# One-hots of a counting sort stored and reloaded, high rows loaded a group ahead, four count buffers, and a later first node piece

## The chip, the cores and the metric

The kernel runs on one core of one Trainium2 chip. A core has five engines that each execute their own queue in order: TensorE (PE, with its weight loads PEld), VectorE (DVE), ScalarE (ACT), GpSimd (POOL) and SyncE (SP, which here issues most plain DMAs). DMAs move the data between DRAM and the on-chip memory; those that gather or scatter rows by an index list are issued by POOL, one instruction for 128 rows. The metric is the device time of one execution in microseconds (us), the median of three runs.

## The reference

A graph layer on 3125 nodes of 256 features. It has three parts:

```
xn = layernorm(x)
x  = x + gnn(xn, edge_attr, src, dst) + mix(xn)      # 103125 edges, sorted by dst
x  = x + ffn(layernorm(x), edge_index)               # 65536 other edges + one loop for each node

gnn:  msg = concat(nodes[src], edge_attr) @ W_message       # 320 -> 256
      agg = segment_sum(msg, dst)
      h = layernorm(relu(agg) + nodes); three-layer MLP with skips; layernorm
mix:  4 layers of (linear attention over all nodes; feed-forward 256 -> 1024 -> 256)
ffn:  h = x @ W_gat (16 columns); e = leaky_relu(a_src[src] + a_dst[dst])
      alpha = softmax of e over the edges of one dst; agg = segment_sum(h[src] * alpha, dst)
      scores = mean over heads of layernorm(agg + b_gat); the two best of 4 experts, softmax
      weighted sum of the experts' MLPs, all four computed densely
```

The 65536 edges of the last part are not sorted. The kernel sorts them by destination itself.

## The kernel before

**Message passing.** The 103125 edges lie as 128 partitions of 806 consecutive edges ("columns"). `gather_chunk` loads the attributes of 8 columns (L494, SP) into one of three buffers `m_run` and lets POOL gather the 128 source rows of each column (L515). `sum_up` (L527, DVE) adds a column to the running sum of its partition, and after the eighth column SP stores the chunk to `run_d` (L532). The chunk's buffer then takes the next gathers. After the last column, `message_nodes` fetches for each tile of 128 nodes the finished sum (`fetch`, L595, POOL, into `aggr`), and `pair` carries two tiles through transposes (L611), the message weights (L619, L620), layer norms and the MLP, in steps ("pieces").

**The sort.** The edges lie as 128 x 512, in 64 groups of GC = 8 positions. A destination is split into a high part (127 bins) and a low part (32 bins).

- `count_group(t)` builds one-hots of the high parts (`oh_hi`, L695) and the low parts (`oh_lo`, L701, made by `low_hots`, 64 KB in f16, three buffers) on DVE; eight matmuls (L716) give each position's count table; ACT casts it into one of two buffers `counts0`, `counts1` (L718); SP stores it to `counts_d` (L719); PE adds it to a table kept for the whole sort (L723). That last matmul is for the group counted one call before.
- `starts` turns the table into the place of each destination's first edge and loads the counts of the first group (`parts`, L732). `edge_ranges`, 25 `ends_tile`, `ends_sum` and `ends_done` find where each node's edges begin and end; `ends_tile` works in a buffer `ends_buf`.
- `place_group(t)` loads the high parts of the group's edges in transposed order, broadcast to all partitions (`hr`, 256 KB, two buffers, L756, SP), compares them with the partition number (`ohT`, L758, DVE), builds the low one-hots once more (`low_hots`, L701), runs a scan over the group's counts (L761) and orders the edges within the group by products of one-hots (L775, ACT's sign into `earlier`). In the next call the matmuls from L781 on (the first reads `oh_lo`), the product `own` and the sum L791 give each edge's number. Every fourth group, `laid` turns numbers into places.
- `send(t)` scatters 128 edges to their places (L805, POOL); there are 512.

**The mix** runs on PE, ACT and DVE beside all of this; `finish` ends it for four tiles, computes the GAT table `tab` (L859) and scatters the rows of a dst (L866, POOL). After it the rows of the sources are fetched in sorted order (L1291, 340 gathers into `rows_c`), and the rest of the last part ends the kernel.

**Order.** The program's text sets each engine's order through a planner's clock, and a scheduler in the compiler may still move what is not pinned. After each step of the mix, `pace(us)` moves the clock on, runs one waiting piece of the node stage, and writes as many columns (later sends) as the clock has room for at one each 1.27 us; columns are pinned in that order. `beside(us)` takes jobs of the sort from a list, each with a cost in planned time. When the last column is written, 24 sends go out and `message_nodes` is called.

```
    def pace(us):
        clock["now"] += us
        if pieces:
            piece()
        ...
        while clock["columns"] < TM and FIRST + COLUMN * (clock["columns"] + 1) <= clock["now"]:
```

Of the kernel before, what the change touches and what calls it, by code (L numbers as in the profile page):

```python
# [11 lines left out]
F16 = mybir.dt.float16  # L12
# [6 lines left out]
P = 128  # L19
# [21 lines left out]
TE = E2 // P  # L41
NEXP = 4
GC = 8
GROUPS = TE // GC
SRC = 4096
LO = 32
# [13 lines left out]
def kernel(ctx: ExitStack, tc: tile.TileContext, a: dict, out: bass.AP):  # L60
# [347 lines left out]
        V.tensor_scalar(above, node_n, -1.0, SRC // 2 - 0.5, op0=ALU.mult, op1=ALU.add)  # L408

    def ends_tile(t):  # L410
        buf = so.tile([P, 8 * P], F16, name="ends_buf", tag="hr", bufs=2)
        at_least = buf[:, 6 * P:7 * P]
        V.tensor_scalar(at_least, row0, start_t[:, t:t + 1], None, op0=ALU.is_ge)
        T.matmul(first_ps[:, t:t + 1], at_least, ones_h, start=True, stop=True, skip_group_check=True)
        le, own = buf[:, :P], buf[:, P:2 * P]
        V.tensor_scalar(le, ids, whole_t[:, t:t + 1], None, op0=ALU.is_ge)
        T.matmul(whole_ps[:, t:t + 1], le, ones_h, start=True, stop=True, skip_group_check=True)
        V.scalar_tensor_tensor(own, ids, prev_t[:, t:t + 1], le, op0=ALU.is_ge, op1=ALU.subtract)
        for k, (c0, c1) in enumerate(((0, TM // 2), (TM // 2, TM))):
            ps = pa.tile([P, 512], F32, name="ps_a")  # L420
            T.matmul(ps[:, :c1 - c0], own, dst_h[:, c0:c1], start=True, stop=True)
            hit = buf[:, 2 * P:2 * P + TM // 2]
            S.activation(hit, ps[:, :c1 - c0], AF.Sign, bias=above[:, t:t + 1], accum_out=cnt2n[:, k, t:t + 1])
# [117 lines left out]


    FIRST, COLUMN, PIECE, EARLY = 52.0, 1.27, 0.9, 24
    clock = {"now": 45.0, "columns": 0, "sent": 0}

    pieces = []

# [4 lines left out]

    def pace(us):
        clock["now"] += us
        if pieces:
            piece()
        pinned = True
        while clock["columns"] < TM and FIRST + COLUMN * (clock["columns"] + 1) <= clock["now"]:
            sum_up(clock["columns"], pinned)
            pinned = False  # L560
            clock["columns"] += 1
            if clock["columns"] == TM:
                while clock["sent"] < min(EARLY, clock["placed"]):
                    send(clock["sent"])
                    clock["sent"] += 1
                for _ in range(len(jobs) - N_JOBS + ENDS):
                    jobs.pop(0)[1]()
                msgs.close()
                message_nodes()
        while (clock["columns"] == TM and clock["sent"] < clock["placed"]  # L570
               and FIRST + COLUMN * (TM + clock["sent"]) <= clock["now"]):
            send(clock["sent"])
            clock["sent"] += 1
# [125 lines left out]
    def low_hots(t):  # L699
        o = so.tile([P, GC, LO], F16, name="oh_lo", bufs=3)  # L700
        V.tensor_tensor(o, low_ids.rearrange("p (o l) -> p o l", o=1).to_broadcast([P, GC, LO]),  # L701
                        lo[:, t:t + GC].rearrange("p (t o) -> p t o", o=1).to_broadcast([P, GC, LO]), op=ALU.is_equal)
        return o

    counts_d = dram.tile([GROUPS, P, LO * (GC + 1)], F16, name="counts_d")
    counted = []
    cnts = [so.tile([P, LO, GC + 1], F16, name=f"counts{k}") for k in range(2)]
    for o in cnts:
        V.memset(o[:, :, 0], 0.0)

    def count_group(t):
        if t < TE:
            ohh, ohl = one_hot(t, hi, P, "oh_hi", 2), low_hots(t)
            ps = pg.tile([P, GC, LO], F32, name="ps_g")
            for i in range(GC):
                T.matmul(ps[:, i, :], ohh[:, :, i], ohl[:, i, :], start=i == 0, stop=i == GC - 1, skip_group_check=True)  # L716
            cnt = cnts[t // GC % 2]
            S.copy(cnt[:, :, 1:].rearrange("p l i -> p i l"), ps)  # L718
            nc.sync.dma_start(counts_d[t // GC, :, :], cnt.rearrange("p l i -> p (l i)"))  # L719
            counted.append((t, cnt))  # L720
        if t:
            t, cnt = counted.pop(0)
            T.matmul(table, ident_h, cnt.rearrange("p l i -> p (l i)"), start=t == 0, stop=t + GC == TE, skip_group_check=True)  # L723

    def split(x, near, rest):

        V.tensor_copy(near, x)
        V.tensor_tensor(rest[:, :, 0], x, near, op=ALU.subtract)
# [6 lines left out]
    def starts():  # L735
        cnt2 = so.tile([P, LO], F32, name="cnt2", tag="base")
        V.tensor_reduce(cnt2, table.rearrange("p (l i) -> p l i", i=GC + 1), AX.X, ALU.add)
        cum2 = so.tile([P, LO], F32, name="cum2", tag="oh_lo", bufs=3)
        V.tensor_tensor_scan(cum2, ones[:, :LO], cnt2, 0.0, op0=ALU.mult, op1=ALU.add)
        ps = pg.tile([P, LO], F32, name="ps_g")  # L740
        T.matmul(ps[:, :1], before, cum2[:, LO - 1:], start=True, stop=True)
        V.tensor_tensor(cum2, cum2, cnt2, op=ALU.subtract)
        base2 = so.tile([P, 1], F32, name="base2")
        V.tensor_copy(base2, ps[:, :1])
        V.tensor_scalar(cum2, cum2, base2, None, op0=ALU.add)
        nc.sync.dma_start(start_d, cum2)
        V.tensor_scalar(cum2, cum2, half, None, op0=ALU.add)
        places.append(parts(0))
        split(cum2, *places[0])

    def place_group(t):

        late = looks.pop() if looks else None
        if t < TE:
            hr = so.tile([P, GC, P], F16, name="hr", bufs=2)
            nc.sync.dma_start(hr.rearrange("p t e -> p (t e)"), row_h[t // GC:t // GC + 1, :].to_broadcast([P, P * GC]))  # L756
            ohT = ohTs[t // GC % 2]
            V.tensor_scalar(ohT[:P - 1], hr[:P - 1], bin_p[:P - 1], 2.0, op0=ALU.is_equal, op1=ALU.mult)  # L758
            ohl = low_hots(t)
            near, run_l = places.pop()  # L760
            V.tensor_tensor_scan(run_l.rearrange("p l i -> p (l i)"), goes.rearrange("p l i -> p (l i)"),  # L761
                                 run_l.rearrange("p l i -> p (l i)"), 0.0, op0=ALU.mult, op1=ALU.add)
            run = so.tile([P, GC, LO], F16, name="run_c", tag=f"counts{t // GC % 2}")
            S.copy(run, run_l[:, :, :GC].rearrange("p l i -> p i l"))
            if t + GC < TE:
                base = so.tile([P, LO], F32, name="base")
                V.tensor_tensor(base, run_l[:, :, GC], near, op=ALU.add)
                places.append(parts(t + GC))
                split(base, *places[0])

            earlier = so.tile([P, GC, P], F16, name="earlier", bufs=2)
            for i0 in range(0, GC, 4):
                ps = pt.tile([P, 4, P], F32, name="ps_t")
                for i in range(4):
                    T.matmul(ps[:, i, :], ohT[:, i0 + i, :], ohT[:, i0 + i, :], start=i == 0, stop=i == 3, skip_group_check=True)  # L775
                S.activation(earlier[:, i0:i0 + 4, :], ps, AF.Sign, bias=slope[:, 2:3], scale=slope[:, 1:2])  # L776
            looks.append((t, ohT, ohl, near, run, earlier))
        if late:
            t, ohT, ohl, near, run, earlier = late
            look = pg.tile([P, GC, LO], F32, name="ps_g")  # L780
            T.matmul(look, all_h, ohl, start=True, stop=False, skip_group_check=True)  # L781
            for k in range(3):
                for i in range(GC):
                    if k == 2:
                        a1, a2 = earlier[:, i, :], ohl[:, i, :]
                    else:
                        a1, a2 = ohT[:P - 1, i, :], run[:P - 1, i, :] if k else near[:P - 1]
                    T.matmul(look[:, i, :], a1, a2, start=False, stop=k == 2, skip_group_check=True)
            own = so.tile([P, GC, LO], F32, name="own_bin", bufs=1)
            V.scalar_tensor_tensor(own, look, float(E2), ohl, op0=ALU.add, op1=ALU.mult)  # L790
            V.tensor_reduce(number[t // SG % 2][:, t % SG:t % SG + GC], own, AX.X, ALU.add)  # L791
            if (t + GC) % SG == 0:
                V.tensor_scalar_mul(number[t // SG % 2], number[t // SG % 2], 0.5)
                laid(place[:, t + GC - SG:t + GC], number[t // SG % 2])
                clock["placed"] = t + GC

    places = []
    looks = []
    SG = 4 * GC
    number = [so.tile([P, SG], F32, name=f"number{i}") for i in range(2)]  # L800

# [900 lines left out]
```

## Time and profile before

| | us |
|---|---|
| three runs | 2485.49, 2495.59, 2499.51; median 2495.59 |
| the profiled execution | 2499.97, of which the span of the trace is 2498.3 |

| stage of the trace (us) | what runs in it |
|---|---|
| 34 to 145 | first gathers and columns, first layer of the mix begins |
| 145 to 340 | the 64 count groups, in three bursts, beside 124 gathers |
| 340 to 496 | starts, ranges, ends; 111 gathers |
| 496 to 1198 | place groups (36 of 64), the mix, 500 gathers; the last column ends at 1200.6 |
| 1198 to 1908 | 512 sends, 25 fetches of sums, the node stage, the other 28 place groups |
| 1908 to 1940 | last feed-forward matmul at 1918.7, the last scatters of the GAT table |
| 1940 to 2498 | 340 gathers of source rows (to 2417) and the tail |

How it is read. A line of the groups gives the source line, the engine, the operation, what it writes and reads, the number of instructions, then busy time and mean duration in ns, then the idle time of the engine just before these instructions and what ended it. For POOL, "issue" is time in which the engine waited for nothing that the profile shows; it comes with every DMA that POOL issues. A line of the waits gives the engine and line that waited, what released it, the sum in us, how often, and the longest. A line of a timeline begins with the start in us and the duration. A line of the windows view gives the stretch, its length, the busy time of PE, PEld, DVE, ACT and POOL, the granted TensorE clock, the busy share of the DMA engines, and GB/s.

### The profile page before, as it was taken

What the parts mean: (1) busy time and instruction counts of PE and PEld (TensorE: products, weight loads), DVE (VectorE), ACT (ScalarE), POOL (GpSimd) and SP (SyncE); (2) the same over time, 40 slices, a digit from 0 to 9 for tenths busy, and PEclk for the clock granted to TensorE, in tenths of its full rate; (3) what the DMA queues carried; (4) which work ended last, traced back from release to release, by engine and by line L of the source; (5) the groups of instructions that cost most, each with busy time, mean ns of one, the idle gap of its engine ahead of it and who ended that gap; (6) DMA issues with size and microseconds to landing.
All of it is one profiled execution on the core that took longest, in us unless ns stands there. A gap on an engine that the chain in (4) does not pass through costs nothing. (4 is left out here: it accounts for less than half of the span.)

```text
span 2498.3 us, 32120 instructions
## 1 busy us (share of the span) xinstructions
PE 2047.1 (82%) x10045; PEld 1417.0 (57%) x10045; DVE 1481.2 (59%) x4506; ACT 1168.8 (47%) x2040; POOL 1723.6 (69%) x1755
## 2 busy tenths in 40 slices
PE   3869778587879998879499988899999698888874
PEld 2656555365556666547276665666676455555544
DVE  7886876677777667678254434656442344444446
ACT  5646555345444444444255656556544132323234
POOL 4575667667767777766777777777776766666652
PEclk9979888797889998889699989999999898999987
DMA  8986778878987877877411112213110121211112
GB/s 256 313 255 215 247 216 274 209 253 258 304 263 260 262 264 238 294 256 247 144 30 37 37 34 55 73 45 82 45 26 8 23 47 21 48 21 31 23 21 61
DMA packets 302237, 361.80 MB, mean 145 GB/s; under 512 B 183324, under 2 KB 249205, under 8 KB 288853
## 3 DMA queue, kind: packets, MB, share of 16 engines
q1 hardware_dynamic: 233061, 244.77, 30.7%
q0 software_dynamic: 68992, 114.85, 16.9%
q8 instruction: 82, 1.34, 0.2%
q14 instruction: 102, 0.84, 0.1%
HBM read 203.45 MB, written 160.11 MB: 146 GB/s over the span
## 5 line engine op out<-in xcount | busy, mean ns | idle before, releaser
L515 POOL DMA_INDIRECT m_run<-xn_d,src_i x806 | 813.8, 1010 | 378.0 <-issue 211.9
L805 POOL DMA_INDIRECT by_dst<-pairs,place x512 | 502.5, 982 | 156.1 <-issue 154.3
L527 DVE SCALAR_TENSOR_TENSOR m_run<-m_run,stay 128x320 f32<-128x320 f32 x805 | 437.6, 544 | 73.4 <-DMA m_run<-xn_d,src_i 61.9
L1291 POOL DMA_INDIRECT rows_c<-tab_d,si x340 | 326.7, 961 | 150.2 <-issue 100.4
L1149 PE MATMUL ps_a<-h,w 128*128 128x512 f32 (+1 forms) x896 | 392.6, 584 | 6.2 <-ACT h L165 6.1
L1160 PE MATMUL ps_a<-w,gT 128*128 128x256 f32 x1600 | 366.3, 383 | 0.0
L1160 PEld LDWEIGHTS ps_a<-w,gT 128*128 128x128 f32 x1600 | 304.0, 192 | 49.1 <-issue 6.1
L1149 PEld LDWEIGHTS ps_a<-h,w 128*128 128x128 f32 x896 | 168.3, 207 | 167.1 <-issue 148.7
L1150 ACT ACTIVATE gT<-ps_a,b 128x512 f32<-128x512 f32 (+1 forms) x224 | 141.0, 637 | 137.9 <-PE ps_a L1149 136.0
L124 ACT ACTIVATE hn<-xm,rstd 128x256 f32<-128x256 f32 x225 | 120.9, 594 | 62.3 <-DVE rstd L120 58.2
L776 ACT ACTIVATE earlier<-ps_t,slope 128x512 f16<-128x512 f32 x128 | 93.9, 772 | 110.8 <-PE ps_t L775 110.4
L1284 DVE SCALAR_TENSOR_TENSOR ps_g<-tile_ids,high_of,ps_g 128x500 f32<-128x500 f32 x60 | 43.8, 740 | 169.4 <-PE ps_g L1283 168.3
L1410 ACT ACTIVATE hf<-ps_a,be 128x512 f32<-128x512 f32 (+1 forms) x112 | 69.9, 640 | 154.3 <-PE ps_a L1408 147.3
L1283 PE MATMUL ps_g<-tab_c,which 128*128 128x500 f32 x120 | 69.0, 700 | 67.0 <-DVE rows_c L1286 64.3
L160 PE MATMUL ps_t<-ident,hn 128*128 128x128 f32 x450 | 83.7, 320 | 47.3 <-ACT hn L124 41.5
L1087 PE MATMUL ps_g<-xm,kr 128*128 128x256 f32 x400 | 109.6, 412 | 11.8 <-ACT kr L1085 11.3
L1061 PE MATMUL ps_a<-wq,h 128*128 128x256 f32 x400 | 100.5, 394 | 20.8 <-ACT kT L1041 12.8
L1029 PE MATMUL ps_a<-h,wk 128*128 128x512 f32 (+1 forms) x224 | 103.7, 598 | 2.7 <-ACT h L165 2.7
L1087 PEld LDWEIGHTS ps_g<-xm,kr 128*128 128x128 f32 x400 | 78.6, 205 | 44.2 <-ACT kr L1085 29.0
L160 PEld LDWEIGHTS ps_t<-ident,hn 128*128 128x128 f32 x450 | 57.5, 159 | 81.3 <-ACT hn L124 59.6
L1138 PE MATMUL ps_a<-co,hT 128*128 128x256 f32 x400 | 99.3, 391 | 0.8 <-DVE co L1129 0.6
L718 ACT CAST counts<-ps_g 128x256 f16<-128x256 f32 x64 | 80.3, 1375 | 41.5 <-PE ps_g L716 21.4
(436 smaller groups left out, 3812.4 us busy)
## 6 DMA issues: line engine op xcount, KB each, us to landing
run_d<-m_run SPq DMA_DIRECT2D x100, 1280.0 KB
m_run<-in_edge_attr_dram SPq DMA_DIRECT2D x95, 256.0 KB
hr<-row_h SPq DMA_DIRECT2D x64, 256.0 KB
m_run<-xn_d,src_i POOLq DMA_INDIRECT x806
w<-in_L_mix_W_dram SPq DMA_DIRECT2D x8, 1024.0 KB
by_dst<-pairs,place POOLq DMA_INDIRECT x512
rows_c<-tab_d,si POOLq DMA_INDIRECT x340
run_d<-rows_c SPq DMA_DIRECT2D x15, 312.0 KB
```

Source lines behind the costliest of these rows:

```text
L124: S.activation(dst, src, AF.Identity, bias=r[:, 1, i:i + 1], scale=r[:, 0, i:i + 1])
L160: T.transpose(ps[:, i * P:(i + 1) * P], src[:, c * P:(c + 1) * P], ident)
L515: last_gather[0] = G.indirect_dma_start(out=m[:, t, :D], out_offset=None, in_=xn_d, in_offset=bass.IndirectOffsetOnAxis(ap=src_i[:, t0 + t ...
L527: add = V.scalar_tensor_tensor(m[:, t, :], before_m, stay[:, c:c + 1], m[:, t, :], op0=ALU.mult, op1=ALU.add)
L805: i = G.indirect_dma_start(out=by_dst, out_offset=bass.IndirectOffsetOnAxis(ap=place[:, t:t + 1], axis=0), in_=pairs0[:, t:t + 1], in_offs ...
L1029: T.matmul(ps[:, :n], att_w[l]["wk"][:, kc, m * P:(m + 1) * P], h1[:, kc, :n], start=kc == 0, stop=kc == 1)
L1061: T.matmul(ps[:, i, :], h1[:, kc, o + i * P:o + (i + 1) * P], att_w[l]["wq"][:, kc, :], start=kc == 0, stop=kc == 1)
L1087: T.matmul(ps_x[:, m, :], kr[:, m * P:(m + 1) * P], xm[:, t, :], start=i == 0 and m == 0, stop=i == len(c) - 1, skip_group_check=True)
L1149: T.matmul(ps[:, :w], ff_w[l]["w1"][:, kc, f * P:(f + 1) * P], h2[:, kc, :w], start=kc == 0, stop=kc == 1)
L1150: S.activation(gT[:, f, :w], ps[:, :w], AF.Gelu, bias=ff_w[l]["b1"][:, f:f + 1])
L1160: T.matmul(ps[:, i, :], gT[:, f, (2 * i0 + i) * P:(2 * i0 + i + 1) * P], ff_w[l]["w2"][:, f, :], start=False, stop=f == FF // P - 1, skip_ ...
L1291: G.indirect_dma_start(out=rows_c[:, t - COLS[j], :], out_offset=None, in_=tab_d, in_offset=bass.IndirectOffsetOnAxis(ap=si[:, t:t + 1], a ...
```

## The change

1. **Low one-hots.** `count_group` also stores its `oh_lo` to a DRAM tile `lows_d` (64 stores of 64 KB, 512 bytes for each partition). `place_group` no longer builds them; they are loaded from there.
2. **High rows.** The load of `hr` leaves `place_group`. A new `ahead_of(t)` loads `hr` and `oh_lo` of one group; `starts` calls it for the first two groups, and `place_group` calls it for the group after the next right after `own`. `ends_buf` uses the buffers of `earlier` instead of those of `hr`.
3. **Count buffers.** Four instead of two (the two new ones share the space of `run`), and the table matmul L723 follows two groups behind the counting instead of one; what is left is added at the end.
4. **Node stage.** When the columns are done, the pieces may start only once the planner's clock has moved on by 1.27 x (24 + 8) = 40.6 us. The pace (52.0 and 1.27) stays.

SP issues 128 more DMAs (1640 to 1768), and DVE 64 fewer one-hots. The order of columns against place groups is the same. Line numbers in the text are those of the kernel before.

```diff
     def ends_tile(t):
-        buf = so.tile([P, 8 * P], F16, name="ends_buf", tag="hr", bufs=2)
+        buf = so.tile([P, 8 * P], F16, name="ends_buf", tag="earlier", bufs=2)
...
     def pace(us):
         clock["now"] += us
-        if pieces:
+        if pieces and clock["now"] >= clock["fetched"]:
             piece()
...
                 message_nodes()
+                clock["fetched"] = clock["now"] + COLUMN * (EARLY + 8)
...
     cnts = [so.tile([P, LO, GC + 1], F16, name=f"counts{k}") for k in range(2)]
+    cnts += [so.tile([P, LO, GC + 1], F16, name=f"counts{k}", tag="run", bufs=2) for k in range(2, 4)]
+    lows_d = dram.tile([GROUPS, P, GC * LO], F16, name="lows_d")
...
-            cnt = cnts[t // GC % 2]
+            cnt = cnts[t // GC % 4]
             S.copy(cnt[:, :, 1:].rearrange("p l i -> p i l"), ps)
             nc.sync.dma_start(counts_d[t // GC, :, :], cnt.rearrange("p l i -> p (l i)"))
             counted.append((t, cnt))
-        if t:
-            t, cnt = counted.pop(0)
-            T.matmul(table, ident_h, cnt.rearrange("p l i -> p (l i)"), start=t == 0, stop=t + GC == TE, skip_group_check=True)
+            nc.sync.dma_start(lows_d[t // GC, :, :], ohl.rearrange("p t l -> p (t l)"))
+        while counted and (len(counted) > 2 or t >= TE):
+            now, cnt = counted.pop(0)
+            T.matmul(table, ident_h, cnt.rearrange("p l i -> p (l i)"), start=now == 0, stop=now + GC == TE, skip_group_check=True)
...
         split(cum2, *places[0])
+        for t in (0, GC):
+            ahead_of(t)
+
+    def ahead_of(t):
+        hr = so.tile([P, GC, P], F16, name="hr", bufs=2)
+        nc.sync.dma_start(hr.rearrange("p t e -> p (t e)"), row_h[t // GC:t // GC + 1, :].to_broadcast([P, P * GC]))
+        ohl = so.tile([P, GC, LO], F16, name="oh_lo", bufs=3)
+        nc.sync.dma_start(ohl.rearrange("p t l -> p (t l)"), lows_d[t // GC, :, :])
+        highs.append((hr, ohl))
...
         if t < TE:
-            hr = so.tile([P, GC, P], F16, name="hr", bufs=2)
-            nc.sync.dma_start(hr.rearrange("p t e -> p (t e)"), row_h[t // GC:t // GC + 1, :].to_broadcast([P, P * GC]))
+            hr, ohl = highs.pop(0)
             ohT = ohTs[t // GC % 2]
             V.tensor_scalar(ohT[:P - 1], hr[:P - 1], bin_p[:P - 1], 2.0, op0=ALU.is_equal, op1=ALU.mult)
-            ohl = low_hots(t)
...
             V.scalar_tensor_tensor(own, look, float(E2), ohl, op0=ALU.add, op1=ALU.mult)
+            if t + 2 * GC < TE:
+                ahead_of(t + 2 * GC)
```

More of the change, by code (lines that the diff above doesn't have):

```diff
@@ L543 @@
     FIRST, COLUMN, PIECE, EARLY = 52.0, 1.27, 0.9, 24
-    clock = {"now": 45.0, "columns": 0, "sent": 0}
+    clock = {"now": 45.0, "columns": 0, "fetched": 0.0, "sent": 0}
     pieces = []
@@ L798 @@
     looks = []
+    highs = []
     SG = 4 * GC
```

## The prediction

> **What bounds the kernel now.** I read the page first.
>
> ```profile
> PE 2047.1 (82%) x10045; PEld 1417.0 (57%) x10045; DVE 1481.2 (59%) x4506; ACT 1168.8 (47%) x2040; POOL 1723.6 (69%) x1755
> L515 POOL DMA_INDIRECT m_run<-xn_d,src_i x806 | 813.8, 1010 | 378.0 <-issue 211.9
> L805 POOL DMA_INDIRECT by_dst<-pairs,place x512 | 502.5, 982 | 156.1 <-issue 154.3
> ```
>
> POOL is busy for 69%, but "issue" is time between two of its DMAs that nothing could fill. A gather costs 1010 + 211.9/806 = 1.27 us with it, a send 1.28 us. The 806 gathers (34 to 1198 us) and then 512 sends (to 1908) follow each other with little else, so POOL's order is the path. Only its waits beyond "issue" can be won: 378.0 - 211.9 = 166.1 us for the gathers, 1.8 for the sends.
>
> Next, POOL's groups by stage: counting (145 to 340), the ranges (340 to 496), the first places (496 to 700), and the stage of the sends (1198 to 1940, last three lines).
>
> ```profile
> L515 POOL DMA_INDIRECT m_run<-xn_d,src_i x124 | 129.8, 1047 | 65.6 <-issue 33.5 <-DVE m_run L527 17.1 <-DMA counts_d<-counts 6.3
> L515 POOL DMA_INDIRECT m_run<-xn_d,src_i x111 | 108.5, 978 | 48.0 <-issue 28.0 <-DVE laid L682 9.8 <-DMA m_run<-xn_d,src_i 8.1
> L515 POOL DMA_INDIRECT m_run<-xn_d,src_i x141 | 141.9, 1007 | 61.6 <-issue 37.6 <-DMA run_d<-m_run 6.7 <-DVE run L761 6.3
> L805 POOL DMA_INDIRECT by_dst<-pairs,place x512 | 502.5, 982 | 156.1 <-issue 154.3 <-DMA by_dst<-pairs,place 0.9 <-DVE rstd L120 0.9
> L595 POOL DMA_INDIRECT aggr<-run_d,sum_i x25 | 24.2, 969 | 15.2 <-issue 5.2 <-PE ps_t L775 4.1 <-DMA run_d<-over,carry_i 3.3
> L866 POOL DMA_INDIRECT tgt_d<-tab,start_i x25 | 23.9, 958 | 16.6 <-DVE tab L859 9.6 <-issue 6.4 <-PE ps_a L1408 0.3
> ```
>
> Beyond issue POOL waits 65.6 - 33.5 = 32.1 us in counting, 20.0 and 24.0 in the next two stages; the same view gives 29.0 for 700 to 1076 and 16.5 for 1076 to 1198. That is 121.6 us, the most that the gathers can give after 145 us. The scatters L866 wait 9.6 us for the last table (L859), because PE's mix chain ends (1918.7 us) after the last send (1907.8).
>
> Last, the waits in counting (us in all, times, longest).
>
> ```profile
> PE sums_ps L723 <- ACT counts L718: 42.4, 46, 3.5
> DVE oh_hi L695 <- PE ps_g L716: 23.2, 32, 1.7
> ACT counts L718 <- DMA counts_d<-counts: 18.2, 13, 3.1
> POOL m_run L515 <- DVE m_run L527: 17.1, 6, 6.8
> ```
>
> PE, executing in order, stands at the table matmul (L723) for the cast of the group just counted; DVE then stands at the next one-hot for PE; column sums queued behind it on DVE come late; their chunk's buffer comes free late; POOL waits.
>
> **Counting: four count buffers, lagged table matmul, low one-hots stored.** The 64 groups run in three bursts (147-196, 221-276, 289-338 us), 151 us, or 2.36 us a group. The change removes the waits of 42.4 (the matmul is two groups behind) and 18.2 (a count buffer returns after four groups, not two). It adds 64 stores of 64 KB on SP and a wait: the low one-hot has three buffers, and one is now free only when its store has landed. DVE would stand there with high one-hots and columns behind it, and POOL behind those. No lows_d store is in the trace; the nearest row is the counts store, which ACT's casts wait for. ACT's timeline and SP's, first column the start:
>
> ```profile
> 169.74 2.50 ACT L718 CAST counts<-ps_g 128x256 f16<-128x256 f32 x2 [1.53 <-DMA counts_d<-counts]
> 167.06 5.52 SPq L719 DMA_DIRECT2D counts_d<-counts  x4
> ```
>
> A cast that waited starts 2.7 us after the issue; over the 13 such waits it is 2.7 to 4.7, median 3.2. Old cycle of a count buffer: cast 1.375 (mean of L718) + one issue 0.35 + 3.2 = 4.9 us, over two buffers 2.45 us a group: the measured 2.36 within 4%. New cycle of a low one-hot: DVE 0.42 (L701) + eight matmuls about 0.7 (PE's timeline has seven in 0.59) + cast 1.375 + two issues 0.7 + 3.2 = 6.4 us, over three buffers 2.13; scaled by 2.36/2.45, 2.05. I put the store behind the cast because SP issues it after the counts store. Saving: 64 x (2.36 - 2.05) = 20 us, of which I take 18 because the first two groups of a burst gain nothing. It goes to POOL, whose 32.1 us come from these bursts. Ends: +32 if POOL becomes the bound; below nothing as soon as the cycle exceeds 3 x 2.36 = 7.1 us, -41 us by the worst rows (rival c). I take 18, since the store is smaller than the counts store and uses the same queue.
>
> The Trainium skill ("DMA: Bandwidth & Descriptors", section "Anatomy of one DMA") gives a DMA a fixed cost of about 2.0 us, mostly the write's receipt, plus bytes over 436 GB/s: an estimated 2.15 us for 64 KB. By that the cycle is 5.35 us and counting would be held by POOL (32 instead of 18, the sum 14 us larger). The trace's 2.7 to 4.7 us, in a stage whose DMA engines are 73% busy, speaks against it.
>
> **High rows ahead.** place_group loaded hr itself; now the load stands a group ahead, the first two at starts, and ends_buf no longer shares hr's buffers. In the trace only one place waits for it: 484 to 496 us, DVE 12.3 us (L758 <- hr) and PE 21.3 (L775 <- ohT). That goes, but DVE next meets at_end_of (10.8 us, L472), which lands at 508 and whose chain is unchanged. PE gains some 20 us there; DVE's 6 us of waits on PE after 518 us vanish. Most POOL waits of 340 to 496 (laid 9.8, m_run 8.1) have other causes. I take 4, ends 0 and 12. The two first rows and their ohT may run as early as the first columns: two 256 KB loads and two 0.49 us operations beside POOL's wait for DVE there: -2, ends -4 and 0.
>
> **Low one-hots reloaded.** L701 goes from the place groups: 34 x 0.412 = 14.0 us of DVE between 496 and 1198, and PE's wait for it (13.8 us in 700 to 1198). 64 loads come in their place, a group ahead like hr; a place group comes each 20 us or so, a load lands within 5 (above), and SP spends 0.3 us on each: nothing on the path as long as the load keeps that lead, and up to 3 us a group where groups are run back to back. POOL's waits on DVE in these stages are 6.3 (run), 20.5 (m_run), 8.6 (bst) and 5.1 (number), 40.5 in all; 14.0 of DVE's 514 busy us frees a part. I take 8, ends 0 and 28.
>
> **First node piece 40.6 planned us later** (1.27 x 32). In 1200 to 1300 us:
>
> ```profile
> L611 PE MATMUL ps_t<-ident,aggr 128*128 128x128 f32 (+1 forms) x12 | 2.7, 351 | 32.0 <-DMA aggr<-run_d,sum_i 31.5 <-ACT aT L613 0.4
> 1198.00:1330.00 132.00, 93.53 (x412) 61.07 (x411) 44.87 (x133) 56.69 (x101) 95.95 (x98) 0.83 0.23 61
> ```
>
> The second line is the windows view (length, busy PE, PEld, DVE, ACT, POOL, PE clock, DMA share, GB/s). PE stands 31.5 us for the first sums, with mix work behind it in its order, and the granted clock sinks to 0.83 in this stage. After, it runs mix work there. PE's chain ends up to 31.5 us sooner against the sends, POOL becomes the end of the stage, and the gain is the scatters' wait, 9.6 us; with the 4.1 for ps_t it would be 14. I take 9, ends 0 and 14. Sends are issued in the same number with the same spacing, only their neighbours (aggr fetches) stand later. The stage from 1940 on (rows_c, 340 DMAs) is unchanged and moves whole.
>
> **Sum**: 18 + 4 - 2 + 8 + 9 = 37 us. Gathers end near 1170 instead of 1198, sends near 1880. The profiled execution took 2499.97 (span 2498.3), so 2463; the median of the three runs, 2495.6, is 4.4 below it, so 2459.
>
> **Rivals.**
> (a) *Counting becomes POOL-bound and DVE's relief counts in full*: 32 + 4 + 20 - 2 + 14 = 68, hence about 2428. For: all POOL waits there trace back to DVE. Against: the store's cycle above. 0.18.
> (b) *The low one-hot's store takes the place of the count store.* If the cycle comes to 7.1 us (landing 3.9, inside the 2.7 to 4.7), counting gains nothing; nor do the places, if DVE was not their limit. Left: about 4 - 2 + 9 = 11, hence 2485, within 0.5%. That high rows were in effect already fetched as early as two buffers allow (one wait in 64 groups) makes the change do less than it says, and belongs here. 0.17.
> (c) *Slower: SP holds the stores.* SP's queue stands at chunk attributes (L494) for run_d stores, 23.1 us in ten waits in counting, 2.3 each. A low store queued behind one, landing in 3.6: 3.2 (one-hot, matmuls, cast, issues) + 3.6 + 2.3 = 9.1, or 3.0 us a group, 0.64 over the 2.36 and so 41 us lost; with the other 19 won, 2518 at the worst and a net loss from a cycle of 8.0 us on (19/64 = 0.3 us a group over 7.1/3). Against: ten waits for 64 groups. 0.14.
>
> The forecast's own case (2440 to 2480) has 0.51. For the range, 0.2 may be left out: (c) and the far part of (a): 2422 to 2496. A run set of this kernel tells about 0.5%, 12.5 us, from no change. Faster: 0.51 + 0.18 = 0.69; same: 0.17; slower: 0.14.
>
> **What would show it.** Right: L723's wait on L718 gone; L701 or L695 in counting waiting for lows_d stores; L515's idle time in counting near 48 instead of 65.6; columns ending near 1170; L611's 31.5 gone and the clock of that stage up; L866's wait on tab gone; the 340 rows_c starting near 1903 instead of 1940 and lasting as long. Wrong: bursts of 2.4 us a group or more, DVE or PE standing at reloaded one-hots in the place groups, sends no longer back to back, or PE's last mix matmul again behind the last send.

## The result and the profile after

The changed kernel takes 2484.18 us (median of 20 runs, 2478.69 to 2494.68), the kernel before 2491.36 (median of 20). The ratio over these runs is 0.9966, with a 95% interval of [0.9955, 0.9977]: faster by 0.34%, or 8.5 us (the two medians differ by 7.2). That is small, but clear of the noise. The forecast was 37 us. The profiled execution of after took 2483.28 us (span 2481.6), 16.7 less than that of before, because the profiled execution of before was 8.6 us above its median.

Lines of after have moved: the counting matmuls are L719, the cast L721, the store of low one-hots L724, the table matmul L727, the low one-hots L702, the transposes of sums L612, the sends L819, the scatters of the GAT table L880. SP issues 681 DMAs in the trace of before and 809 in that of after, so the 128 more are there, although not at the totals given with the change.

The page of after; the two lines of POOL answer to those of before:

```profile
PE 2058.5 (83%) x10045; PEld 1417.6 (57%) x10045; DVE 1465.3 (59%) x4444; ACT 1156.3 (47%) x2029; POOL 1723.1 (69%) x1755
L515 POOL DMA_INDIRECT m_run<-xn_d,src_i x806 | 810.8, 1006 | 370.5 <-issue 213.0
L819 POOL DMA_INDIRECT by_dst<-pairs,place x512 | 505.7, 988 | 156.1 <-issue 153.7
```

The gathers now wait 370.5 - 213.0 = 157.5 us beyond "issue" instead of 166.1. POOL's groups in counting (145 to 340), the first places (496 to 700), 700 to 1076, and, the last two lines, 1198 to 1940:

```profile
L515 POOL DMA_INDIRECT m_run<-xn_d,src_i x119 | 123.7, 1040 | 72.0 <-issue 31.7 <-DVE m_run L527 27.0 <-DVE oh_hi L696 9.6
L515 POOL DMA_INDIRECT m_run<-xn_d,src_i x147 | 148.3, 1009 | 55.3 <-issue 38.7 <-DMA m_run<-xn_d,src_i 5.8 <-DVE number L804 3.4
L515 POOL DMA_INDIRECT m_run<-xn_d,src_i x279 | 276.1, 990 | 98.1 <-issue 74.3 <-DVE m_run L527 9.0 <-DVE xm L1177 6.0
L596 POOL DMA_INDIRECT aggr<-run_d,sum_i x25 | 24.9, 998 | 10.6 <-issue 7.0 <-DMA run_d<-over,carry_i 3.3 <-PE ps_a L636 0.3
L880 POOL DMA_INDIRECT tgt_d<-tab,start_i x25 | 24.3, 973 | 7.6 <-issue 7.0 <-DVE low_of L1278 0.3 <-DVE tab L873 0.3
```

Counting became worse: 119 gathers instead of 124, waits of 40.3 us beyond "issue" instead of 32.1. The next stages became better (16.6 instead of 24.0, 23.8 instead of 29.0), and the scatters no longer wait for the table. Why counting did not gain is in its waits and in PE's timeline (start, duration):

```profile
DVE oh_hi L696 <- PE ps_g L719: 40.3, 36, 4.5
PE sums_ps L727 <- ACT counts L721: 26.3, 35, 1.4
DVE oh_lo L702 <- DMA lows_d<-oh_lo: 3.2, 6, 1.1
```

```profile
158.46 0.62 PE L719 MATMUL ps_g<-oh_lo,oh_hi 128*128 128x32 f16 x8
159.14 0.28 PE L727 MATMUL sums_ps<-counts,ident_h 128*128 128x288 f16 x1
160.49 0.28 PE L727 MATMUL sums_ps<-counts,ident_h 128*128 128x288 f16 x1 [1.07 <-ACT counts L721]
160.61 0.62 PE L719 MATMUL ps_g<-oh_lo,oh_hi 128*128 128x32 f16 x8
162.65 0.40 PE L727 MATMUL sums_ps<-counts,ident_h 128*128 128x288 f16 x1 [1.43 <-ACT counts L721]
165.91 0.68 PE L719 MATMUL ps_g<-oh_lo,oh_hi 128*128 128x32 f16 x8 [2.86 <-DVE oh_lo L702]
```

Groups are numbered from 0. The eight matmuls of group 5 (158.46) are followed by the table matmuls of groups 4 and 5, those of group 6 (160.61) by that of group 6. The text puts the table matmul two groups behind; the compiler's scheduler put it ahead of the next group's matmuls for 38 of the 64 groups, one group behind for 21, and two behind for 4. The last group has no next one. (In the kernel before, 53 stood one group behind, as the text has it, and 10 ahead of the next group.) So PE still stands for a cast, now that of the group that it has just counted, and DVE's next high one-hot stands behind PE longer than before (40.3 us instead of 23.2). First to last cast take 196.7 us instead of 190.1. Counting comes in bursts, so this time includes pauses. Without the two longest (26.2 and 13.7 us before, 12.0 and 10.2 after) the other 61 steps from one cast to the next take 2.46 us each before and 2.86 after.

### The profile page after: what moved, and what is told of

It reads as the page before. It is cut to its first block, busy times and chain, and to the rows that moved or that the text cites. A ratio compares the mean times of both kernels' runs of the same rounds, so it can differ in the third digit from the quotient of the medians.

```text
span 2481.6 us, 32288 instructions
## 1 busy us (share of the span) xinstructions
PE 2058.5 (83%) x10045; PEld 1417.6 (57%) x10045; DVE 1465.3 (59%) x4444; ACT 1156.3 (47%) x2029; POOL 1723.1 (69%) x1755
## 5 line engine op out<-in xcount | busy, mean ns | idle before, releaser
L515 POOL DMA_INDIRECT m_run<-xn_d,src_i x806 | 810.8, 1006 | 370.5 <-issue 213.0
L819 POOL DMA_INDIRECT by_dst<-pairs,place x512 | 505.7, 988 | 156.1 <-issue 153.7
L1075 PE MATMUL ps_a<-wq,h 128*128 128x256 f32 x400 | 103.2, 398 | 25.9 <-ACT kT L1055 17.1
L721 ACT CAST counts<-ps_g 128x256 f16<-128x256 f32 x64 | 82.2, 1331 | 50.8 <-PE ps_g L719 39.0
L1075 PEld LDWEIGHTS ps_a<-wq,h 128*128 128x128 f32 x400 | 76.0, 197 | 49.9 <-ACT kT L1055 19.1
```

The source lines that it names most:

```text
L515: last_gather[0] = G.indirect_dma_start(out=m[:, t, :D], out_offset=None, in_=xn_d, in_offset=bass.IndirectOffsetOnAxis(ap=src_i[:, t0 + t ...
L819: i = G.indirect_dma_start(out=by_dst, out_offset=bass.IndirectOffsetOnAxis(ap=place[:, t:t + 1], axis=0), in_=pairs0[:, t:t + 1], in_offs ...
L1075: T.matmul(ps[:, i, :], h1[:, kc, o + i * P:o + (i + 1) * P], att_w[l]["wq"][:, kc, :], start=kc == 0, stop=kc == 1)
```

## The experiments

Theory 1: the compiled order undoes the lag of the table matmul, and this is what counting lost. Theory 2: the stores that hold the low one-hot's buffers set the cycle. After the first run without a stall they became theory 3 (each limit hides the other, so that only removing both helps) and theory 4 (DVE's own order and load is the limit anyway).

**Chips.** The eighteen runs of this section fell on chips of two kinds. On two of them the kernel before took 2497 us; on five others 3647 to 3716 us (called stalling chips below). There DVE, ACT and POOL are as busy as elsewhere, but the engines stand for several us at a time with no release that this core's profile shows ("issue", "remote"). Ratios from these five hold only there. What they still show is the order of counting: which waits exist, and how long it takes against other kernels on such chips.

**The table matmul pinned.**

```diff
-                T.matmul(ps[:, i, :], ohh[:, :, i], ohl[:, i, :], ...)
+                last_count[0] = T.matmul(ps[:, i, :], ohh[:, :, i], ohl[:, i, :], ...)
...
-            T.matmul(table, ident_h, ...)
+            with tc.issue_after(last_count[0].ins):
+                T.matmul(table, ident_h, ...)
```

> The changed kernel, with each table matmul (L727) pinned behind the eight matmuls of the group counted two calls later, as the text of the program means it. Theory 1 (order): in the compiled order of the changed kernel most table matmuls stand right behind their own group's matmuls, so PE still stands for the cast (26.3 us in 35 waits, and DVE's high one-hots behind it 40.3 us in 36); with the pin those 26.3 us go, counting drops from about 2.5 us a group to 2.1 or less, the columns end some 15 to 20 us sooner, and the whole is 0.6 to 0.8% below the changed kernel. Theory 2 (store): the low one-hots' buffers, held until their stores land, set the cycle; then the pin moves the time by less than 0.2% and the wait turns into one of DVE or PE for lows_d or oh_lo.

On a stalling chip: 1.0129 [1.0101, 1.0156]. The same kernel again:

> The pinned table matmuls once more, because on the chip of the first four runs all kernels took half as long again (before: 3705 us) and their engines stood for several us with no release in the profile. On a chip where the kernel before takes about 2490 us. Theory 1 (order): PE's wait for the cast at the table matmul (26.3 us in the changed kernel) goes, counting comes to 2.1 us a group or less, the columns end 15 to 20 us sooner than in the changed kernel, and the time is 0.989 to 0.991 of the kernel before. Theory 2 (store): 0.995 to 0.998 as the changed kernel, with DVE or PE standing for the low one-hots.

On a chip without stalls: 0.9927 [0.9903, 0.9950], 2478.55 us. Its order is two groups behind for 62 of the 64 groups (the last two follow at the end). Its waits in counting, with the counting matmuls now at L720:

```profile
PEld L720 <- DVE oh_lo L702: 35.9, 27, 5.7
PE ps_g L720 <- DVE oh_lo L702: 26.5, 17, 5.5
DVE oh_hi L696 <- PE ps_g L720: 18.7, 24, 2.5
DVE oh_lo L702 <- DMA lows_d<-oh_lo: 15.1, 14, 2.3
```

No line of the table matmul's wait is left, as theory 1 expected, and DVE's wait for PE is less than half of the changed kernel's. But PE now stands 26.5 us for low one-hots (5.8 in the changed kernel), which DVE holds back 15.1 us for their stores (3.2). First to last cast take 191.0 us (2.76 us a step, without the two longest pauses of 12.6 and 10.3), and POOL starts 122 gathers in the stage. The last gather ends at 1186.9 us, as in the changed kernel (1187.2), and not the 15 to 20 us sooner that theory 1 expected. One wait took the place of the other; neither theory alone is right. The better ratio of this kernel is therefore not explained by the columns of its trace.

**No store and no reload of the low one-hots.** The store is left out of `count_group`, the load out of `ahead_of`, and `place_group` builds them again.

```diff
-            nc.sync.dma_start(lows_d[t // GC, :, :], ohl.rearrange("p t l -> p (t l)"))
...
-            hr, ohl = highs.pop(0)
+            hr = highs.pop(0)
...
+            ohl = low_hots(t)
```

> The changed kernel without the store and reload of the low one-hots: place groups build them again on DVE as the kernel before did; high rows ahead, four count buffers and the later first piece stay. Theory 2 (store): counting gains 15 us or more, since no buffer waits for a landing; the places lose about 8 of it again (14 us of DVE work before the last column), so the whole is 0.2 to 0.5% below the changed kernel. Theory 1 (order): the compiled order still has the table matmuls right behind their own groups, counting stays at about 2.4 to 2.5 us a group, and the whole is equal or up to 0.3% slower.

> The changed kernel without the store and reload of the low one-hots, on a chip like that of the pinned run. In the changed kernel the places gain some 10 us from the missing one-hots; here they should lose it (14 us of DVE before the last column). Theory 1 (order is what holds counting): table matmuls still stand behind their own groups, PE waits some 25 us for casts, counting stays as in the changed kernel, and the time is 0.998 to 1.001 of the kernel before. Theory 2 (stores hold counting): counting gains 10 us or more and the time is 0.993 to 0.996.

> The changed kernel without the store and reload of the low one-hots, table matmuls where the scheduler puts them. Theory 3: PE keeps its wait for the casts (25 to 45 us), counting stays at 185 us or more from first to last cast, and the places lose their gain: 0.998 to 1.002 of the kernel before. Stores alone as the limit: counting 180 us or less and 0.994 to 0.997.

All three fell on stalling chips: 1.0071 [1.0042, 1.0101], 1.0108 [1.0073, 1.0143], 1.0057 [1.0024, 1.0090]. PE's wait for the casts at the table matmul is there in each (44.4, 35.6 and 40.5 us in all).

**Both edits.**

> Both edits: table matmuls pinned two groups behind, low one-hots neither stored nor reloaded. Theory 1 (order): like the pin alone in counting (2.0 to 2.1 us a group), and in the places up to 8 us slower than the pin alone. Theory 2 (store): like the run without store alone. If each of the two limits hides the other, only this run shows the gain in counting, 15 to 30 us.

> Table matmuls pinned two groups behind, and no low one-hot stored or reloaded. The pinned run showed PE's 26 us at the table matmul gone and 26 us (and 36 us of weight loads) for the low one-hots in its place, behind stores that DVE waited for 15 us. Theory 3 (each limit hides the other): only with both gone does counting shorten, to 2.1 us a group or less, 120 gathers of the counting stage become 130 or more by 340 us; the places lose about 10 us again, and the time is 0.990 to 0.994. Theory 4 (DVE's own order and load is the limit in counting): counting keeps 2.4 us a group, and the time is 0.998 to 1.001.

> Table matmuls pinned two groups behind, and the low one-hots neither stored nor reloaded. The run with eight places showed 0.9867 of the kernel before, with counting from 151 to 325 us. Theory 3 (the table matmul's order and the stores each hide the other): without stores counting shortens as much (first to last cast 175 to 180 us against 197 in the changed kernel); the places lose the 14 us of DVE relief again, some 10 us on the path before the last column and some 5 after it; together 0.991 to 0.995. If counting is not shorter than 190 us, the stores were not the second limit.

Stalling chips again: 1.0084 [1.0060, 1.0107], 1.0050 [1.0019, 1.0081], 1.0019 [0.9985, 1.0052], and a fourth run with the same expectation (e10_pin_nostore) 1.0035 [1.0003, 1.0067].

**The pin, and eight places for low one-hots.** Stores and reloads stay; two buffers of `earlier`, free during counting, hold four groups each.

```diff
-            ohh, ohl = one_hot(t, hi, P, "oh_hi", 2), low_hots(t)
+            if t // GC % 4 == 0:
+                four[0] = so.tile([P, 4, GC, LO], F16, name="low_four", tag="earlier", bufs=2)
+            ohh, ohl = one_hot(t, hi, P, "oh_hi", 2), four[0][:, t // GC % 4, :, :]
+            V.tensor_tensor(ohl, ...)      # as in low_hots
```

> The pinned kernel with eight places for low one-hots in counting instead of three (two buffers of earlier, unused then, hold four groups each; a buffer returns when its four stores have landed). Stores and reloads stay. Theory 3: the waits for the stores go, counting shortens to 2.1 us a group or less, the places keep their gain, and the time is 0.983 to 0.988, the best of all. Theory 4: counting keeps 2.4 us a group and the time is 0.992 to 0.995, as the pinned kernel.

On stalling chips 1.0081 [1.0045, 1.0117], and in three more runs 1.0063 [1.0033, 1.0093], 1.0083 [1.0052, 1.0115], 1.0065 [1.0035, 1.0096] (e11_pin_lo8, e13_pin_lo8, e14_pin_lo8). Then on a chip without stalls:

> Table matmuls pinned two groups behind, and eight places for low one-hots in counting instead of three (two buffers of earlier, unused then, hold four groups each; a buffer returns when its four stores have landed). Stores and reloads stay. On the stalling chips the counting of this kernel (first to last cast) took 204 to 213 us against 250 to 269 with the changed kernel's counting. Theory 3 (the table matmul's order and the stores each hide the other): on a chip without the stalls counting shortens to 2.1 us a group or less, 130 gathers or more start in the stage from 145 to 340 us instead of 119 to 124, and the time is 0.983 to 0.988 of the kernel before. Theory 4 (DVE's own order and load is the limit in counting): counting keeps 2.4 us a group and the time is 0.992 to 0.995, as the pinned kernel.

2465.64 us, 0.9867 [0.9842, 0.9893]. It beats both kernels and lies in the range of theory 3. POOL's group in counting, the casts (min/median/max duration in ns, first and last start), and waits that are left in counting (the counting matmuls are now L725, the cast L727, the low one-hots L721):

```profile
L515 POOL DMA_INDIRECT m_run<-xn_d,src_i x130 | 142.5, 1096 | 52.0 <-issue 34.4 <-DVE m_run L527 10.0 <-DVE xm L1160 3.6
L727 ACT CAST counts<-ps_g x64: 1252/1322/1693, 151.4 to 325.3; 128x256 f16<-128x256 f32 x64
PE ps_g L725 <- DVE low_four L721: 20.9, 15, 4.1
PE ps_g L725 <- ACT counts L727: 11.9, 14, 4.0
DVE oh_hi L696 <- PE ps_g L725: 10.1, 13, 2.1
```

130 gathers, waits of 52.0 - 34.4 = 17.6 us beyond "issue" (40.3 in the changed kernel, 32.1 before), casts over 173.9 us, no wait for a cast at the table matmul nor for a store of low one-hots. Without its two longest pauses (27.2 and 12.5 us) a step takes 2.20 us, a little over the 2.1 of theory 3. The pin alone left counting at 191.0 us, the pin with eight places brought it to 173.9: this fits theory 3. Its other half, that more places without the pin would gain nothing, is not shown. The counting matmuls still wait for DVE's low one-hots (20.9 us), the part of theory 4 that is true, and for casts (11.9 us). Not all of the shorter waits reached the total: the gathers of this stage took 1096 ns each instead of 1047, while the DMA engines were busy for 85% instead of 73%, so that 130 of them took 6.4 us longer; no run shows why. From the trace of before to this one, the last gather ends 19.4 us sooner (1178.3 instead of 1197.7), and the stretch from there to the first source row is 10.7 us shorter.

First to last cast in us, by kernel (on the stalling chips, the second row is always the changed kernel with the early piece):

| counting as in | without stalls | stalling chips |
|---|---|---|
| before | 190.1 | |
| changed, and changed with the early piece | 196.7, 196.6 | 255.0, 269.1, 249.9 |
| pinned | 191.0 | 250.6 |
| no store | | 237.0, 245.8, 217.5 |
| pinned, no store | | 227.1, 220.5, 208.2, 202.1 |
| pinned, eight places | 173.9 | 211.1, 204.0, 210.0, 212.7 |

On the stalling chips too, the kernels with both limits gone are the quickest in counting, with the two ways of removing the stores' hold about alike. But there the two limits are not equals. In two sets of runs on one chip, leaving out the stores alone shortened counting from 255.0 to 237.0 us and from 269.1 to 245.8, while the pin alone gave 250.6 in the first set; the pin on top of it gave another 9.9 and 25.3 us. One kernel differs there by up to 28 us between chips and sets, so only the direction is to be read. It speaks against the strict form of theory 3, by which the stores alone would give nothing. Whether taking the stores' hold alone would do on a chip without stalls is open: no such run fell there.

**The first node piece as early as before.**

```diff
-                clock["fetched"] = clock["now"] + COLUMN * (EARLY + 8)
+                clock["fetched"] = clock["now"]
```

> The changed kernel with the node stage's first piece as early as before; all else stays. By the prediction's term the wait of PE for the first sums (31.5 us) comes back, the scatters wait about 9 us for the GAT table again, and the whole is 9 us (0.36%) slower than the changed kernel: then most of the measured gain is this part's. If the term is wrong the time is within 0.1% of the changed kernel.

> The changed kernel with the node stage's first piece as early as before. By the prediction's term PE stands again for about 31 us for the first sums, the scatters wait about 9 us for the GAT table, and the time is 0.36% more than the changed kernel: 1.000 of the kernel before. If the term is wrong: 0.996 to 0.997, as the changed kernel.

Stalling chips: 1.0059 [1.0038, 1.0081], 1.0060 [1.0032, 1.0088], and 1.0043 [1.0009, 1.0076] in e12_nolate. Then on a chip without stalls:

> The changed kernel with the node stage's first piece as early as before. By the prediction's term PE stands again for about 31 us for the first sums, the scatters wait about 9 us for the GAT table, and the time is 0.36% more than the changed kernel: 1.000 of the kernel before. If the term is wrong: 0.996 to 0.997, as the changed kernel.

2491.15 us, 0.9976 [0.9961, 0.9991]. The wait is back (28.6 us), and the granted clock of 1198 to 1330 us is as it was before the change (0.84 and 0.83); the last line is that stage in the changed kernel (1.00).

```profile
L612 PE MATMUL ps_t<-ident,aggr 128*128 128x128 f32 (+1 forms) x18 | 3.8, 328 | 29.8 <-DMA aggr<-run_d,sum_i 28.6 <-ACT h L165 1.3
L880 POOL DMA_INDIRECT tgt_d<-tab,start_i x25 | 24.1, 966 | 12.2 <-issue 6.7 <-DVE tab L873 4.9 <-PE ps_a L1422 0.3
1198.00:1330.00 132.00, 94.61 (x412) 61.61 (x411) 44.77 (x132) 56.99 (x101) 97.19 (x98) 0.84 0.26 71
1198.00:1330.00 132.00, 125.37 (x633) 90.69 (x632) 63.15 (x186) 72.89 (x135) 98.83 (x100) 1.00 0.21 53
```

From the last gather's end to the first source row (rows_c) there are 742.1 us before, 732.7 changed, 735.4 here. So of the 9.4 us that this stage gained, the later piece gave 2.7 in these traces; the scatters waited only 4.9 us for the table without it, not 9.6. The other 6.7 came with the rest of the change. That it was because the place groups of this stage also lost their one-hots is likely, but not shown. By the ratios (0.9976 and 0.9966) the later piece is worth 0.1%, and the intervals overlap.

## Why the prediction was wrong

The step that failed is the counting term: +18 us forecast. In the trace it is 32.1 - 40.3 = -8.2 us. The prediction took the lag of the table matmul from the program's text ("the matmul is two groups behind") and cancelled PE's 42.4 us with it. In the compiled order the lag was there for only 4 of the 64 groups; 26.3 us of the wait remained, and DVE's wait for PE rose by 17.1. That the order made these waits is shown: pinned to the order of the text, the table matmul does not wait in this stage, and DVE's wait for PE falls from 40.3 to 18.7 us. The order is not the whole reason why counting gained nothing, since it took 191.0 us with the pin too.

The prediction also misread where the 42.4 us came from: not the cast of the group just counted. In the kernel before, 39 of the 46 waits (35.7 us) are at table matmuls that stand one group behind, so that PE stood for the cast of the group before. There the compiled order followed the text.

Its cycle of 6.4 us for a low one-hot's buffer was too short as well. A landing was sized about right: in the pinned run, the 14 low one-hots that waited for a store started 2.3 to 6.4 us after its issue, median 3.3, where 3.2 was taken (the 13 waits for the counts stores before the change, measured again in the trace, have 2.7 to 5.0 and median 3.3, where the prediction has 2.7 to 4.7 and 3.2). (The Trainium skill, "DMA: Bandwidth & Descriptors", section "Anatomy of one DMA", would give an estimated 2.15 us, by a fit made for DMAs that GpSimd issues; SP issued these, and all of them took longer.) What was too small is the part ahead of the store: for those 14 it was issued 2.1 to 6.8 us after its low one-hot started, median 4.2, where the prediction has 6.4 - 3.2 = 3.2. The sum had no room for the columns and the mix that stand between these steps in the engines' orders. Their whole cycle has a median of 7.6 us, and the prediction itself says that above 7.1 nothing is gained. Counting took 191.0 us from first to last cast where 64 groups were to save 20. With eight places, POOL's waits fall by 32.1 - 17.6 = 14.5 us: near the forecast's 18, but with another kernel.

Point by point, from the two traces:

| term | forecast | measured |
|---|---|---|
| counting | +18 | -8.2 (waits beyond issue, 32.1 to 40.3) |
| high rows ahead, and low one-hots reloaded (340 to 1198) | +4 and +8 | 89.5 to 71.3: +18.2 |
| two first rows and ohT early | -2 | about 0 (gather 50 starts at 113.1 instead of 113.6) |
| later first piece, sends to rows_c | +9 | +9.4, of which 2.7 by the piece itself |
| rows_c to the end | 0 | -3.2 (558.5 to 561.7) |
| sum | +37 | +16.2; span 16.7 |

The first source row is fetched at 1919.9 us, where the prediction has 1903 (before: 1939.8). The sum in the traces is larger than the 8.5 us of the ratio. The changed kernel and the one with the early piece have the same instructions in the same order up to the last gather, and their traces, from two chips, end it at 1187.2 and 1199.2 us. Twelve us between two executions are thus no sign of a difference. In the second of these traces POOL waits 87.2 us beyond "issue" from 340 to 1198 us, so that by it the places gained only 2.3 us and not 18.2: that the two place terms (+12 forecast) were right is not shown. Nor is the later piece's +9 confirmed by the 9.4, of which only 2.7 is its own; that the sizes agree is luck. What is beyond this scatter is the wait at the table matmul in counting (26.3 us in one, 23.5 in the other, 42.4 before, none when pinned), the time of counting (196.7 and 196.6 us), and the ratios.

The rival that came nearest in time was (b), a gain of 11 us; its mechanism, a cycle at the landing's slow end, was not what held counting in the changed kernel (3.2 us of waits for landings). In the pinned run the cycle did exceed 7.1 us (15.1 us of such waits, and the 7.6 above), but through the part ahead of the store and not through a slow landing. Rival (c)'s long holds of SP did not decide: in counting SP stood 12.6 us for `run_d` stores in the changed kernel and 23.1 before. None of the rivals had the scheduler in it.

## What to carry to other kernels

A lag that is written in the program's text is only a wish as long as a scheduler may move the instruction: read the compiled order of the engine in question, or pin the instruction, before taking its wait out of a sum. When a buffer gets a new last reader (here a store), its places are held until that reader is done, and the wait that was removed can return under another name unless it gets more of them; here the pin with three places left counting at 191.0 us, and the pin with eight (no number between was run) brought it to 173.9 and the kernel to 0.9867. And a stage's change of 10 us is not read from one pair of traces when two traces of the same order differ by 12.

## What the runs showed that was not expected

On five of the seven chips of the experiments the same kernels took about half as long again (the kernel before 3647 to 3716 us instead of 2497). The page of the pinned kernel on one of them, and two of its largest waits:

```profile
PE 2255.4 (60%) x10045; PEld 1514.7 (40%) x10045; DVE 1462.1 (39%) x4444; ACT 1158.0 (31%) x2027; POOL 1690.6 (45%) x1755
L515 POOL DMA_INDIRECT m_run<-xn_d,src_i x806 | 794.6, 986 | 831.3 <-issue 231.8
```

```profile
DVE own_bin L803 <- remote: 218.4, 18, 24.5
ACT y_all L1438 <- remote: 157.6, 10, 20.6
```

The work of DVE, ACT and POOL is about what it is elsewhere (1465, 1156 and 1723 us in the changed kernel), and PE's is longer (2255.4 us instead of 2058.5) at a mean granted clock of 0.77 instead of 0.91. But DVE stands up to 24.5 us at one instruction with no releaser on this core. On these chips the variants were slower than the kernel before, by up to 1.3% (one not clearly), and the version that was best elsewhere by 0.6% to 0.8%. The cause of the stalls, and why they turn the order round, was not found.
